# A graph diffusion with a routed feed-forward layer: the order of loads, stores and zeroing in SyncE's queue

## The chip, the cores and the metric

The kernel runs on one core of one Trainium2 chip. The metric is the device time of one execution in microseconds; of the kernel before, three runs are shown, and one further execution was recorded by the hardware profiler. Engines: PE is TensorE, DVE is VectorE, ACT is ScalarE, POOL is GpSimd, SP is SyncE. SP computes nothing here: it reads a few registers and issues most of the DMAs, strictly in the order of its queue.

## The reference

There are 3125 rows (nodes) of 256 numbers and 103,125 edges. First a linear graph diffusion of six steps, then a layer of eight experts, of which each row uses two. Cut to what matters:

```python
x = x + gnn(layernorm(x))          # silu(h @ W_in.T + b_in), 6 diffusion steps, @ W_out.T + b_out
xn = layernorm(x) * gamma + beta
top_vals, top_idx = top_k(xn @ Wr + br, 2)
w = softmax(top_vals)
for e in range(8):
    h = gelu(xn @ W1[e] + b1[e])   # 256 -> 512
    y = y + (h @ W2[e] + b2[e]) * w_full[..., e, None]
x = x + y
```

One diffusion step is `term = segment_sum(term[src], dst) * inv_deg / i`, and the six terms and the start are added up.

## The kernel before, in words

**First step.** The edges are made into a dense matrix of 25 row blocks of 128 x 3200 (`build_tile`, L647 to L687): DVE compares, PE multiplies (`pa`), ACT writes the block, and SP copies it to DRAM (`adj`, L686). In the same loop (L718) each block is multiplied with the start vector (`pd`, L727), and `finish` scales and adds. `last`, what `finish` returns, is an instruction of DVE.

In the first ten rounds of this loop SP also issues a DMA that writes 640 KB of zeros into the DRAM tensor `ys` (`nought`, L721): `ys` has one row of results for each of the two experts of each node, and every row that is read later must hold a number. These DMAs wait for nothing in the loop, and the scheduler that puts the instructions of each engine in order has set them ahead of the first block's copy.

**Steps two to six** (L1106): the blocks come back from DRAM one by one, and PE multiplies them, 25 blocks a step.

**Routing.** During the last step each block of 128 rows is normalised, the two best experts are found, and POOL scatters the row twice into the DRAM tensor `xs`, a list for each expert (`route`, L900). `lists_end` cuts the lists into pieces of 256 rows, 27 pieces in all, and orders them so that pieces whose rows come early in the node order come first.

**The experts' stage** (`experts`, L1017, called at L1130). Piece i passes through these steps:

- `load(i)` (L1024): SP reads the piece's first row and its expert into registers, and issues five DMAs: `xr` (256 rows and, in a 257th column, the row of `ys` for each result; 257 KB), `w1_sb` and `w2_sb` (512 KB each), `b1_sb` (2 KB) and `b2_sb` (128 KB). These tiles have three buffers each, so xr of piece i+2 can be loaded when nothing reads xr of piece i-1 any more. The last reader is the scatter of piece i-1, which takes its row numbers from it.
- `turned`: PE transposes the piece into `px` (L1045), DVE copies it to `xt` (L1048).
- `hidden`: PE multiplies with W1 into `ph` (L1056), ACT applies gelu (L1058).
- `results`: for each half of 128 rows PE multiplies with W2 into `py` (L1065), DVE adds the bias into `y` (L1068; three buffers), and POOL scatters the 128 rows into `ys` (L1069).

The loop at L1077 stands in this order: hidden(i), turned(i+1), results(i), load(i+2). PE's order in a round is thus `ph` of i, `px` of i+1, `py` of i.

**Sums.** `READY` (L57) names four checkpoints: before piece 10 the results of the nodes' blocks 0 to 4 are complete, before piece 16 those of blocks 5 to 9, before piece 21 blocks 10 to 14, before piece 24 blocks 15 to 19. If the order of the pieces doesn't allow it, a flag (`rare`) is set and all is done again behind the stage. In the rounds of the checkpoints `results_of` (L994) loads the five blocks' results, two DMAs of 640 KB (`got0`, `got1`; L1000). It reads `ys`, which the scatters write. The scatters among themselves are told apart by `dram_disjoint_views`; the load of `got` is not, so it waits for all scatters before it in the program, and the next scatter behind it in the program waits for the load. `summed` (L1008) then does two DVE instructions for a block (L1011, L1013) and a store to the output (L1015), two blocks a round in rounds that are no checkpoint. Blocks 20 to 24 are loaded when the last piece is done (4 whole blocks and the last of 53 rows, so four DMAs), and their stores are shared by SP and ACT.

The order of each engine's queue is set by a scheduler that looks at readiness. `tc.issue_after(ins)` is a block in which every instruction that goes to the queue of `ins`'s own engine is put behind `ins` in that queue; it makes no wait, and it says nothing about other engines.

## Time and profile before

| what | us |
|---|---|
| three runs: median (lowest to highest) | 1333.0 (1332.65 to 1334.83) |
| the profiled execution | 1329.78 |
| its span, first to last instruction | 1328.0 |
| mean granted clock of TensorE | 0.971 of full |
| PE busy | 1231.4 (93%) |
| DVE busy | 622.2 (47%) |
| ACT busy | 347.4 (26%) |
| POOL busy | 115.5 (9%) |
| `pd` of steps two to six (L1121), PE busy | 713.5 |
| `py` (L1065) and `ph` (L1056), PE busy | 100.4 and 99.4 |
| `ys<-nought`, ten DMAs of 640 KB, issue to landing | 10.4 (median) |
| `got<-ys`, eight DMAs of 640 KB, issue to landing | 5.8 (median) |
| `xr<-xs`, 27 DMAs of 257 KB, issue to landing | 2.8 (median) |

The page says for each engine how long it was busy, for each group of instructions how often it ran and what ended the idle time before it, and for each DMA how long it took from issue to landing. A share of busy time is a mean over stages with different limits. The views of the trace say more: the waits of an engine and who ended them, the timeline of a stretch, and for a stretch the busy times, the clock that TensorE was granted (PEclk, 1.00 is full) and what the DMA engines moved. Where an instruction waits for several things the profile names the one that came last by its own reckoning, which can be the wrong one.

### The profile page before, as it was taken

Reading aid. Unit: us, or ns where it says so; the run is one execution under the profiler, and the core shown is the slowest. Engines: PE = TensorE matmul, PEld = TensorE weight load, DVE = VectorE, ACT = ScalarE, POOL = GpSimd, SP = SyncE. Lnnn points to the kernel's source line nnn. Section 1 sums busy time; section 2 is a strip of 40 time slices with the busy share of each in tenths; the row PEclk is TensorE's granted clock in tenths of the full one; section 3 lists DMA queues with packets and bytes.
Section 4 is the critical chain, followed back from the end, with each engine's and each line's share of the span. In section 5 each row is a group of like instructions: output and inputs, shape, how many; then the busy total and the mean of one; then the engine's idle time right before and its main releaser. Section 6 shows DMA issues by size and latency. Waiting matters only on the chain. (4 is left out here: it accounts for less than half of the span.)

```text
span 1328.0 us, 16605 instructions
## 1 busy us (share of the span) xinstructions
PE 1231.4 (93%) x6190; PEld 1017.5 (77%) x6190; DVE 622.2 (47%) x1587; ACT 347.4 (26%) x534; POOL 115.5 (9%) x141
## 2 busy tenths in 40 slices
PE   3899999998999999999999999999999829998983
PEld 2678888887888888888888888887777618877872
DVE  5759999995344443333222222236555422122232
ACT  4656676664000000000000000002222202222220
POOL 2000000000000000000000000000333222221221
PEclk9899999999999999999999999999999959999996
DMA  9204444345988888888888888887888276787892
GB/s 302 95 11 192 190 165 196 159 202 227 357 292 294 293 292 295 293 293 295 295 295 295 296 294 297 297 291 276 289 288 287 89 187 223 223 254 252 256 297 99
DMA packets 91059, 326.08 MB, mean 246 GB/s; under 512 B 12013, under 2 KB 61052, under 8 KB 71768
## 3 DMA queue, kind: packets, MB, share of 16 engines
q1 hardware_dynamic: 82588, 307.71, 65.2%
q0 software_dynamic: 5280, 14.54, 3.3%
q10 hardware_dynamic: 3100, 2.66, 0.7%
q8 instruction: 51, 0.84, 0.2%
q14 instruction: 40, 0.33, 0.1%
HBM read 256.44 MB, written 67.63 MB: 244 GB/s over the span
## 5 line engine op out<-in xcount | busy, mean ns | idle before, releaser
L1121 PE MATMUL pd<-t,blk 128*128 128x512 f32 (+1 forms) x3125 | 713.5, 388 | 4.0 <-DMA blk<-adj 4.0
L1121 PEld LDWEIGHTS pd<-t,blk 128*128 128x128 f32 x3125 | 575.2, 188 | 121.8 <-issue 4.3
L695 DVE SCALAR_TENSOR_TENSOR term<-pd,inv_deg,low 128x256 f32<-128x256 f32 x150 | 72.4, 482 | 406.2 <-ACT low L693 406.0
L693 ACT ACTIVATE low<-pd,inv_deg 128x256 f32<-128x256 f32 x150 | 71.2, 475 | 642.5 <-PE pd L1121 575.5
L681 ACT CAST blk<-pa 128x800 fp32r<-128x800 f32 x98 | 146.5, 1645 | 12.1 <-PE pa L677 12.1
L727 PE MATMUL pd<-t,blk 128*128 128x512 f32 x625 | 145.9, 389 | 0.0
L727 PEld LDWEIGHTS pd<-t,blk 128*128 128x128 f32 x625 | 115.4, 188 | 23.3
L666 DVE TENSOR_TENSOR right<-steps,place 128x800 bf16<-128x800 f16 (+3 forms) x245 | 128.1, 579 | 3.3 <-PE pa L677 3.3
L1065 PE MATMUL py<-w_sb,ht 128*128 128x256 f32 x432 | 100.4, 387 | 0.0
L1056 PE MATMUL ph<-xt,w_sb 128*128 128x256 f32 x432 | 99.4, 383 | 0.8 <-DVE xt L1048 0.8
L677 PE MATMUL pa<-right,left 128*128 128x200 bf16 (+3 forms) x980 | 98.9, 254 | 0.9 <-ACT blk L681 0.9
L677 PEld LDWEIGHTS <-left 128*128 128x128 bf16 x980 | 83.4, 97 | 13.8 <-issue 4.6
L1056 PEld LDWEIGHTS ph<-xt,w_sb 128*128 128x128 f32 x432 | 83.0, 193 | 12.7 <-DVE xt L1048 1.2
L1058 ACT ACTIVATE ht<-ph,b_sb 128x256 f32<-128x256 f32 x108 | 50.9, 474 | 158.5 <-PE ph L1056 153.6
L1065 PEld LDWEIGHTS py<-w_sb,ht 128*128 128x128 f32 x432 | 82.1, 195 | 10.6
L657 DVE TENSOR_TENSOR left<-steps,lane 128x2560 bf16<-128x2560 f16 x49 | 72.8, 1485 | 1.2 <-PE pa L677 1.1
L769 POOL IOTA lane_f<- 128x1 f32 x1 | 0.1, 138 | 840.7 <-PE pd L1121 840.7
L1069 POOL DMA_INDIRECT ys<-y,xr x54 | 53.0, 982 | 175.9 <-DVE y L1068 106.0
L1048 DVE COPY xt<-px 128x512 f32<-128x512 f32 x27 | 18.6, 691 | 97.0 <-PE px L1045 78.8
L900 POOL DMA_INDIRECT xs<-xg,to x50 | 48.9, 977 | 104.5 <-DVE m L839 37.9
L701 DVE TENSOR_TENSOR acc<-acc,term 128x256 f32<-128x256 f32 x125 | 52.5, 420 | 0.9
L1068 DVE TENSOR_TENSOR y<-py,b_sb 128x256 f32<-128x256 f32 x54 | 22.9, 424 | 61.2 <-PE py L1065 61.0
(233 smaller groups left out, 606.9 us busy)
## 6 DMA issues: line engine op xcount, KB each, us to landing
blk<-adj SPq DMA_DIRECT2D x125, 1600.0 KB, 6.7
adj<-blk SPq DMA_DIRECT2D x25, 1600.0 KB, 5.2
w_sb<-in_w_dram SPq DMA_DIRECT2D x54, 512.0 KB, 5.5
xr<-xs SPq DMA_DIRECT2D x27, 257.0 KB, 2.8
ys<-nought SPq DMA_DIRECT2D x10, 640.0 KB, 10.4
got<-ys SPq DMA_DIRECT2D x8, 640.0 KB, 5.8
b_sb<-in_b_dram SPq DMA_DIRECT2D x27, 128.0 KB, 5.2
out_dram<-got SPq DMA_DIRECT2D x22, 128.0 KB, 5.2
```

Of the source, the lines that this page charges most:

```text
L657: nc.vector.tensor_tensor(left.rearrange("p k a l u -> p (k a) l u"), steps[:, None, :P, :].to_broadcast([P, nl, P, 2]), lane[:, h, :, :]. ...
L666: nc.vector.tensor_tensor(r, steps[:, None, :m, :].to_broadcast([P, HALF // 2, m, 2]), place[:, h, k, :].rearrange("p (a u) -> p a u", u=2 ...
L677: nc.tensor.matmul(pa[:, u, lo * NT:hi * NT], left[:, k, a, :, u], right[k][:, a, :, u], start=(k == 0), stop=(k == CK - 1), skip_group_ch ...
L681: nc.scalar.copy(by_dst[:, q:q + 2 * W, :].rearrange("p (u q) i -> p u q i", u=2), pa[:, :, :W * NT].rearrange("p u (q i) -> p u q i", i=NT))
L693: nc.scalar.activation(low, pd[:, D:], AF.Copy, scale=inv)
L695: put = nc.vector.scalar_tensor_tensor(term, pd[:, :D], inv, low, op0=ALU.mult, op1=ALU.add)
L701: put = nc.vector.tensor_add(acc[:, j, :], acc[:, j, :], term)
L727: nc.tensor.matmul(pd[:, :n], blk[:, i * P:(i + 1) * P], t0[:, i, :n], start=(i == 0), stop=(i == NT - 2), skip_group_check=True)
L1056: nc.tensor.matmul(ph, got[1][:, k, q * P:(q + 1) * P], xt[:, k, :], start=(k == 0), stop=(k == 1))
L1065: nc.tensor.matmul(py, ht[:, q, h * P:(h + 1) * P], got[2][:, q, :], start=(q == 0), stop=(q == HT - 1))
L1069: nc.gpsimd.indirect_dma_start(ys_at[2 * min(i, NSLOT) + h], bass.IndirectOffsetOnAxis(ap=got[0][:, h, D:].bitcast(U32), axis=0), y, None)
L1121: nc.tensor.matmul(pd[:, :n], blk[:, i * P:(i + 1) * P], old[:, i, :n], start=(i == 0), stop=(i == NT - 2), skip_group_check=True)
```

## The change

There are four parts.

1. In the first step the zeroing DMAs move from rounds 0 to 9 to rounds 2 to 11, and stand in a block `tc.issue_after(last.ins)`.
2. In the experts' loop `load(i + 2)` moves from the end of the round to its start, and the loads of results at a checkpoint come next, ahead of hidden(i). `load` also returns its last DMA (of `b2_sb`), and `results` its last DVE addition (`y`).
3. The sums of a round stand in two order blocks: the DVE part behind `y` of the round, the stores on SP behind the last DMA of the newest load.
4. Blocks 20 to 24 are loaded in pairs (20 and 21, 22 and 23, 24 alone), `got0` from SP's queue and `got1` from ACT's, and the sums of a pair follow its loads.

```diff
     for j in range(NT):
-        if j < 10:
+        if 2 <= j < 12:
             n = 2 * YK // 10
-            nc.sync.dma_start(ys[j * n:(j + 1) * n, :].rearrange("(a p) d -> p a d", p=P),
-                              nought[:, None, :].to_broadcast([P, n // P, D]))
+            with tc.issue_after(last.ins):
+                nc.sync.dma_start(ys[(j - 2) * n:(j - 1) * n, :].rearrange("(a p) d -> p a d", p=P),
+                                  nought[:, None, :].to_broadcast([P, n // P, D]))
...
-    def results_of(sums, a, b):
+    def results_of(sums, a, b, on=(nc.sync, nc.sync)):
...
-            nc.sync.dma_start(
-                got[:, :full - a, :],
-                ys[k * YK + a * P:k * YK + full * P, :].rearrange("(t p) d -> p t d", p=P))
+            if full > a:
+                on[k].dma_start(
+                    got[:, :full - a, :],
+                    ys[k * YK + a * P:k * YK + full * P, :].rearrange("(t p) d -> p t d", p=P))
             if full < b:
-                nc.sync.dma_start(got[:LAST, full - a, :], ys[k * YK + full * P:k * YK + N, :])
+                on[k].dma_start(got[:LAST, full - a, :], ys[k * YK + full * P:k * YK + N, :])
...
-                nc.sync.dma_start(b2_sb, b2[ds(e, 1), :].to_broadcast([P, D]))
-                return xr, w1_sb, w2_sb, b1_sb, b2_sb
+                d = nc.sync.dma_start(b2_sb, b2[ds(e, 1), :].to_broadcast([P, D]))
+                return xr, w1_sb, w2_sb, b1_sb, b2_sb, d.ins
...
-                for i in range(a, b):
-                    ht = hidden(got[0], xt)
-                    if i + 1 < b:
-                        xt = turned(got[1])
-                    for n, t in READY if sums else ():
-                        if i == n:
-                            both = results_of(sums, gone, t)
-                            left += [(both, gone, q) for q in range(gone, t)]
-                            gone = t
-                    results(i, got[0], ht)
-                    got = got[1:]
-                    if i + 2 < b:
-                        got.append(load(i + 2))
-                    if i not in [n for n, _ in READY]:
-                        for one in left[:2]:
-                            summed(*one, nc.sync)
-                        left = left[2:]
-                if sums:
-                    both = results_of(sums, gone, NT)
-                    for one in left:
-                        summed(*one, nc.sync)
-                    for q in range(gone, NT):
-                        summed(both, gone, q, nc.scalar if q % 2 else nc.sync)
+            for i in range(a, b):
+                if i + 2 < b:
+                    got.append(load(i + 2))
+                for n, t in READY if sums else ():
+                    if i == n:
+                        both = results_of(sums, gone, t)
+                        left += [(both, gone, q) for q in range(gone, t)]
+                        gone = t
+                ht = hidden(got[0], xt)
+                if i + 1 < b:
+                    xt = turned(got[1])
+                y = results(i, got[0], ht)
+                got = got[1:]
+                if i not in [n for n, _ in READY]:
+
+                    with tc.issue_after(y.ins), tc.issue_after(got[-1][-1] if got else y.ins):
+                        for one in left[:2]:
+                            summed(*one, nc.sync)
+                    left = left[2:]
+            if sums:
+                for one in left:
+                    summed(*one, nc.sync)
+                for q in range(gone, NT, 2):
+                    both = results_of(sums, q, min(q + 2, NT), (nc.sync, nc.scalar))
+                    for t in range(q, min(q + 2, NT)):
+                        summed(both, q, t, nc.scalar if t % 2 else nc.sync)
```

The arithmetic is the same. Every DMA of before is there with its size, except that the last results are cut into pairs.

More of the change, by code (lines that the diff above doesn't have):

```diff
@@ L1067, in results @@
                     y = ffn.tile([P, D], F32, name="y")
-                    nc.vector.tensor_add(y, py, got[4])
+                    put = nc.vector.tensor_add(y, py, got[4])
                     nc.gpsimd.indirect_dma_start(
@@ L1071, in results @@
                         bass.IndirectOffsetOnAxis(ap=got[0][:, h, D:].bitcast(U32), axis=0), y, None)
-            got, gone, left = [], 0, []
-            if True:
-                got = [load(i) for i in range(a, min(a + 2, b))]
-                xt = turned(got[0])
-                for i in range(a, b):
-                    ht = hidden(got[0], xt)
-                    if i + 1 < b:
-                        xt = turned(got[1])
-                    for n, t in READY if sums else ():
-                        if i == n:
-                            both = results_of(sums, gone, t)
-                            left += [(both, gone, q) for q in range(gone, t)]
-                            gone = t
-                    results(i, got[0], ht)
-                    got = got[1:]
-                    if i + 2 < b:
-                        got.append(load(i + 2))
-                    if i not in [n for n, _ in READY]:
+                return put
@@ new lines, in experts @@
+            gone, left = 0, []
+            got = [load(i) for i in range(a, min(a + 2, b))]
+            xt = turned(got[0])
+            for i in range(a, b):
[13 more added lines that the diff above has]
+                    with tc.issue_after(y.ins), tc.issue_after(got[-1][-1] if got else y.ins):
```

## The prediction

> **What bounds the kernel now.** I read the page first: PE is busy for 93% of the span, but the chain of waits reaches back only to 1077.8 us, so the diffusion before it is PE from end to end. Then the sums per stretch: from 1089.9 (first `ph`) to 1306.0 (end of the last `py`) stands the experts' stage, 27 pieces of 256 rows. Then the waits of that stage, and the timeline at the first place where PE stops in it.

> ```profile
> span 1328.0 us, 16605 instructions
> ...
> PE px L1045 <- DMA xr<-xs: 29.9, 5, 17.6
> ```

> The second line is from the waits (in all, times, longest): 17.6 us are the start of the stage, the other 12.3 us are four stops, at pieces 12, 18, 23 and 26, each the piece loaded just behind a pair of `got` loads. The timeline at the first (start, duration, engine; in brackets the idle time before it and its releaser):

> ```profile
> 1168.52 0.60 PE L1045 MATMUL px<-ident,xr 128*128 128x128 f32 x4
> ...
> 1171.53 0.95 SPq L1000 DMA_DIRECT2D got<-ys  x2
> ...
> 1172.68 0.38 SPq L1030 DMA_DIRECT2D xr<-xs  x1
> ...
> 1178.68 1.00 POOL L1069 DMA_INDIRECT ys<-y,xr  x1 [11.75 <-DVE got L1011]
> ...
> 1178.79 1.09 PE L1045 MATMUL px<-ident,xr 128*128 128x128 f32 x4 [2.76 <-DMA xr<-xs]
> 1179.67 4.62 PE L1065 MATMUL py<-w_sb,ht 128*128 128x256 f32 x16
> ...
> 1183.85 0.38 SPq L1030 DMA_DIRECT2D xr<-xs  x1
> ...
> 1187.58 0.60 PE L1045 MATMUL px<-ident,xr 128*128 128x128 f32 x4
> ```

> Two things are to be seen. First, SP waits for the scatter of piece 9 (landed 1171.48), issues `got`, and only then xr of piece 12, which lands behind 1.3 MB, 2.9 us too late. Second, the scatter of piece 10, whose y was ready at 1171.3, goes out at 1178.68: it writes `ys`, which the `got` loads read, so it waits until they have landed. The row names a DVE instruction, but got1 (6.0 us from its issue at 1171.96) had landed at 1177.96, and at all four places POOL starts 0.7 to 0.9 us after got1 lands. In the built programs, before and after alike, that scatter waits for both `got` loads. And xr of piece 13 (1183.85) waits for that scatter, since it takes its buffer.

> PE's undisturbed step is 7.345 us ((1168.52 - 1102.41)/9, `px` to `px`). Against it the four places lose: piece 10's 2.93 + 1.45 (px 12 and then px 13), piece 16's 3.70, piece 21's 3.07, piece 24's 3.34 + 1.69 = **16.2 us** in all. The 1.45 and 1.69 are TensorE at half clock. Windows (PE busy, PEclk, DMA share, GB/s):

> ```profile
> 1174.87:1178.28 3.41, 1.16 (x6) 1.00 1.09 363
> 1178.28:1181.69 3.41, 2.90 (x9) 0.50 1.04 342
> 1226.07:1229.48 3.41, 1.50 (x9) 1.00 1.07 365
> ```

> After a stretch of 3.41 us with 1.16 us of PE work the next is at 0.50; after one with 1.50 it is not.

> **The change, part by part.**

> *Zeroing.* The ten `nought` DMAs are put into an order block behind `last`, a DVE instruction. Such a block orders only what is queued on that instruction's own engine, and these are on SP. In the built order they stand where they stood, places 9 to 18 of SP's queue, with the same waits. 0 us. (Had they moved, the gathers beside them, 6.2 and 7.2 us to landing, could at best come near the 2.4 us of a quiet scatter: some 4 us each.)

> *Loads ahead of `got` at pieces 10, 16 and 21.* SP is released at the same moment S (1171.53, 1220.99, 1260.35), because load(i+2) waits for the same scatter as `got` did. xr lands at about S + 2.8 (median of all xr), before its need at S + 4.3, 3.3, 4.5: the stop at px 12, 18 and 23 goes. What is late next is the scatter held by `got`. `got` now follows five loads (1.41 MB). In all 2.76 MB flow; the rows

> ```profile
> 1171.50:1174.00 2.50, 2.50 (x13) 2.19 (x13) 0.00 (x0) 0.47 (x1) 0.00 (x0) 1.00 0.39 82
> 1174.00:1177.90 3.90, 2.03 (x10) 1.45 (x8) 1.85 (x5) 1.42 (x3) 0.00 (x0) 1.00 1.09 367
> ```

> say 0.2 MB in the first 2.5 us and then 0.365 MB/us: 2.5 + 7.0, and 0.2 to land, so got1 lands at **S + 9.7** (before: S + 6.4). Ends: 8.5 if the queue's transfers overlap more than in the rows; 10.4, when the last of the same transfers landed before (1181.9). Then the chain, each step from a row of before: +0.8 POOL's release, +1.3 to the scatter's second half (1178.68 to 1179.99), +2.7 its landing (2.4/2.7/3.4 around 1270), +0.1 issue, +2.7 xr (2.7 and 2.6 at 1232 and 1272), +0.1 to PE: px of piece 13, 19, 24 at **S + 17.4**. Undisturbed they are due at 1183.21, 1231.65 and 1272.20. Late by 5.7, 6.7, 5.6 = 18.0 us. In the built order two of the eight matmul pairs of `py` stand ahead of exactly these three `px`, and fill 0.86 us of each stop (3.46/4): 15.4 us.

> *Half clock.* Each of these stops leaves PE idle for 4.7 to 5.9 us. [...] the rows show 1.45 and 1.69, and PE may come back in mid-window: I take 1.5, ends 0.6 and 2.4. Three times: 4.5 us.

> So pieces 10, 16, 21 cost 15.4 + 4.5 = 19.9 us, where they cost 4.4 + 3.7 + 3.1 = 11.1: **+8.8 us**.

> *Piece 24.* No load follows piece 26's, so nothing waits for the held scatter on PE's side: px 26 comes in time, and 5.0 us go. Part comes back on DVE and POOL: got1 lands at about S + 10.9 (S = 1284.62; there the last load of the set landed at S + 11.8), the scatter of 24 goes out at S + 11.7 and lands 3 us later, y of 25 (second half) waits for its buffer until then, two tiles' sums (4 x 0.43) stand before y of 26, and the last scatter lands at about S + 22.5, before at S + 26.0 (1310.65). **-3.5 us**, ends -1.5 and -5.

> *Sums behind y and the load, stores behind.* In the order block they do stand there. SP's stores wait for sums that end about 2 us after y, and the load behind them waits for a scatter until about 3 us later: hidden. At the end SP's last two stores wait for sums that end about 2 us after y of 26, and the scatter needs 4.2 us: hidden; if not, some 0.5 us.

> *Last tiles in pairs, half of them from ACT's queue.* The tail's row:

> ```profile
> 1312.14 9.15 DMA got<-ys
> ...
> 1316.00:1319.50 3.50, 0.00 (x0) 0.00 (x0) 1.54 (x5) 0.00 (x0) 0.00 (x0) 0.50 0.07 23
> ```

> For 3.5 us the DMA moves 23 GB/s, where 2 us earlier it moved over 340: the two 53-row loads run on one DMA engine, and the final sum waits for the second. The change starts whole tiles sooner, but these 109 kB stay. [...] Were ACT's 53 rows on another engine, 54 kB/23 GB/s = 2.4 us would go, and the row cannot exclude it. I take 0, ends -3 and +1.

> **Sum**: 8.8 - 3.5 + 0 = +5.3 us. The profiled execution is 1329.78 us (span 1328.0 and 1.8 around it), so 1335.1; the median of the runs shown is 3.2 us higher, at 1333.0, and there it is **1338 us**.

> **Rivals.**
> *The held scatter comes free earlier.* If the `got` bytes pass between the loads instead of behind them, got1 lands by S + 7.5. Then px 13, 19 and 24 are 3.5, 4.5 and 3.4 us late, less 2.6 for the `py` in front: 8.8, and with one drop of the clock 10.3, against 11.1. With -3.5: **1329 us**, faster. It decides where got1 lands before about S + 8. For it: scatters did land between loads. Against: before, xr landed 0.7 us after got1 at piece 10, 257 kB at 0.365 MB/us, as in one line.
> *The stops simply go.* -16.2 + 1.5 at piece 24: **1318 us**. It needs a scatter that doesn't wait for `got`; four held scatters (1178.68, 1227.97, 1267.88, 1293.23) speak against it.
> *The clock stays down longer.* Two windows at half rate at each stop, and got1 at S + 10.4: +2.1 and +4: **1344 us**.
> That the zeroing isn't moved is in the sum already.

> **Chances.** Slow chain (1334 to 1342) 0.62; clock down longer 0.10; scatter free earlier 0.18; stops gone 0.06; moved zeroing or a tail on two engines on top, 0.04. What a measurement can tell from no change is 0.2%, 2.7 us. Slower 0.68, within 0.16, faster 0.16. The range takes in the early scatter and most of the long clock: 1328 to 1344.

> **What would show it.** Right: idle before px 13, 19 and 24 of some 5 us, released by xr, none at 12, 18, 23 and 26; POOL's scatter of pieces 10, 16, 21 some 3 us later than before, counted from S; PEclk 0.50 after each stop. Wrong: these scatters within 8 us of S, or a stop elsewhere; zeroing issued after 60 us; the 23 GB/s stretch gone from the tail.

## The result and the profile after

| | us |
|---|---|
| kernel before, four runs: median (lowest to highest) | 1332.83 (1330.45 to 1334.83) |
| changed kernel, four runs | 1347.32 (1344.43 to 1348.32) |
| ratio, 95% interval | 1.0106 (1.0083 to 1.0129) |
| span of the profiled execution, before and after | 1328.0 and 1346.0 |
| granted clock of TensorE, before and after | 0.971 and 0.963 |

The change makes the kernel 1.1% slower. Lines of the changed kernel lie two or more higher than before's: `got` is L1002, `xr` L1032, `px` L1047, `py` L1067, `y` L1070, the scatter L1071. First two of the waits in the profile after (in all, times, longest):

```profile
PE px L1047 <- DMA xr<-xs: 39.9, 4, 18.3
DVE y L1070 <- DMA ys<-y,xr: 29.5, 5, 9.1
```

PE's wait was 29.9 us in five places before. Of the 39.9 us, 18.3 are the start of the stage, so three stops hold 21.6 us where four held 12.3. The timeline around the first of them (start, duration, engine; in brackets the idle time before it and what ended it):

```profile
1173.35 0.38 SPq L1032 DMA_DIRECT2D xr<-xs  x1
...
1176.16 1.00 SPq L1002 DMA_DIRECT2D got<-ys  x2
...
1177.83 0.60 PE L1047 MATMUL px<-ident,xr 128*128 128x128 f32 x4
...
1185.18 1.03 PE L1067 MATMUL py<-w_sb,ht 128*128 128x256 f32 x4
...
1187.06 0.96 POOL L1071 DMA_INDIRECT ys<-y,xr  x1 [18.16 <-DMA got<-ys]
1188.32 0.96 POOL L1071 DMA_INDIRECT ys<-y,xr  x1 [0.31 <-issue]
1189.58 0.42 DVE L1070 TENSOR_TENSOR y<-py,b_sb 128x256 f32<-128x256 f32 x1 [8.95 <-DMA ys<-y,xr]
...
1190.83 0.38 SPq L1032 DMA_DIRECT2D xr<-xs  x1
...
1193.77 1.09 PE L1047 MATMUL px<-ident,xr 128*128 128x128 f32 x4 [7.57 <-DMA xr<-xs]
```

The load of piece 12 now goes first (at S = 1173.35, when SP is released), and `px` of piece 12 at 1177.83 has no bracket: the old stop is gone. `got` follows at 1176.16, and its second half, `got1`, lands at 1186.29. Only then can POOL scatter piece 10 (1187.06), when its second half has landed SP can reload that piece's `xr` buffer (1190.83), and `px` of piece 13 stands at 1193.77 where it was due at 1185.18.

The held scatter keeps a second thing, which the prediction saw only at piece 24: the buffers of `y`. There are three of them, and DVE stands 8.95 us before `y` of piece 11's second half (1189.58), 29.5 us in five places in all; before, DVE has no such wait. It ends before `px` of piece 13 and so does not set the stop here.

Now the stretches of that checkpoint, first two for the DMA, then five in steps of 3.41 us for the clock, which falls at 1188.46 and rises at 1198.70, three such steps apart (length, busy time of PE, PEld, DVE, ACT, POOL, then PEclk, DMA share, GB/s):

```profile
1178.00:1180.50 2.50, 2.50 (x15) 2.24 (x14) 0.99 (x2) 0.47 (x1) 0.00 (x0) 1.00 0.81 254
1183.00:1186.50 3.50, 3.21 (x15) 2.47 (x13) 0.00 (x0) 1.74 (x4) 0.00 (x0) 1.00 0.20 66
1185.10:1188.51 3.41, 1.11 (x6) 0.62 (x4) 0.00 (x0) 0.47 (x1) 1.15 (x2) 0.99 0.01 5
1188.51:1191.92 3.41, 0.00 (x0) 0.00 (x0) 2.00 (x5) 0.00 (x0) 2.80 (x3) 0.50 0.33 117
1191.92:1195.33 3.41, 1.56 (x6) 1.50 (x7) 0.43 (x1) 0.00 (x0) 0.10 (x1) 0.50 0.98 302
1195.33:1198.74 3.41, 3.41 (x9) 2.69 (x9) 0.68 (x2) 0.00 (x0) 0.96 (x1) 0.51 0.93 264
1198.74:1202.15 3.41, 3.41 (x17) 3.00 (x17) 2.00 (x5) 1.06 (x3) 0.96 (x1) 1.00 1.05 349
```

The transfers run at 254 GB/s and end in a tail of 66 GB/s, where before's rows had 363 to 367. And three stretches, not one, are at half clock, two of them with PE at work; at the other two stops it is three and two.

### The profile page after: what moved, and what is told of

Its sections match the earlier page's. It is cut to its first block, busy times and chain, and to the rows that moved or that the text cites. A ratio compares the mean times of both kernels' runs of the same rounds, so it can differ in the third digit from the quotient of the medians.

```text
span 1346.0 us, 16605 instructions
## 1 busy us (share of the span) xinstructions
PE 1235.1 (92%) x6190; PEld 1020.8 (76%) x6190; DVE 623.0 (46%) x1587; ACT 347.5 (26%) x534; POOL 114.9 (9%) x141
## 5 line engine op out<-in xcount | busy, mean ns | idle before, releaser
L681 ACT CAST blk<-pa 128x800 fp32r<-128x800 f32 x98 | 146.5, 1647 | 12.1 <-PE pa L677 12.1
L1067 PE MATMUL py<-w_sb,ht 128*128 128x256 f32 x432 | 103.7, 395 | 0.0
L1067 PEld LDWEIGHTS py<-w_sb,ht 128*128 128x128 f32 x432 | 84.3, 200 | 11.4
L1071 POOL DMA_INDIRECT ys<-y,xr x54 | 52.6, 974 | 195.9 <-DVE y L1070 96.5
L1070 DVE TENSOR_TENSOR y<-py,b_sb 128x256 f32<-128x256 f32 x54 | 22.9, 425 | 88.0 <-PE py L1067 58.4
L1047 PE MATMUL px<-ident,xr 128*128 128x128 f32 x108 | 18.5, 297 | 39.9 <-DMA xr<-xs 39.9
## 6 DMA issues: line engine op xcount, KB each, us to landing
ys<-nought SPq DMA_DIRECT2D x10, 640.0 KB, 10.5
```

What stands on the lines that cost most here:

```text
L681: nc.scalar.copy(by_dst[:, q:q + 2 * W, :].rearrange("p (u q) i -> p u q i", u=2), pa[:, :, :W * NT].rearrange("p u (q i) -> p u q i", i=NT))
L1067: nc.tensor.matmul(py, ht[:, q, h * P:(h + 1) * P], got[2][:, q, :], start=(q == 0), stop=(q == HT - 1))
L1071: nc.gpsimd.indirect_dma_start(ys_at[2 * min(i, NSLOT) + h], bass.IndirectOffsetOnAxis(ap=got[0][:, h, D:].bitcast(U32), axis=0), y, None)
```

## The experiments

They ran in five sets, each with the kernel before beside them: e1 to e4; e5, e6, e7 and after_again; e8, e9, e10 and e6_again; e11 and e12; e13. The kernel before took 1352, 1329, 1333, 1353 and 1349 us, and in the three sets near 1350 the experts' stage begins some 18 us later. Why is not shown; it is not the chip alone, since 1329 and 1353 bear the same chip number. So each time is given as a ratio to the kernel before in the same set.

### The changed kernel again, and the order alone

**after_again** is the changed kernel, unchanged, beside others of these runs.

> The changed kernel as it is, for a profile and a ratio on the same chip as the others: ratio 1.0106 within 0.002, stops at px 13, 19, 24 of 6.4 to 7.7 us, got1 landing at S + 12.5 to 13.3.

Ratio 1.0114 (1.0098 to 1.0131); `px` 13, 19 and 24 are 9.0, 8.2 and 7.3 us late; from S to the held scatter it takes 14.0, 12.8 and 12.5 us.

**e1_got_first**: only the order at a checkpoint is put back.

```diff
-                if i + 2 < b:
-                    got.append(load(i + 2))
                 for n, t in READY if sums else ():
...
+                if i + 2 < b:
+                    got.append(load(i + 2))
```

> The changed kernel, with one thing undone: at a checkpoint the two loads of results stand ahead of load(i+2) again. Theory (the results behind the load land late, the scatter of the checkpoint's piece waits for them, and load(i+3) waits for that scatter): the idle of PE moves back from px of pieces 13, 19, 24 (7.6, 7.6, 6.4 us) to px of 12, 18, 23, 26 (about 2.9, 3.7, 3.1, 3.3 us), the scatter goes out about S + 7 instead of S + 13.7, and the time is that of the kernel before, 1333 (1329 to 1337). Rival (the other parts, zeroing, order of the sums, tail in pairs, cost some of the 14.5 us): the time stays above 1340.

Ratio 0.9995 (0.9982 to 1.0008). Its timeline at the first checkpoint:

```profile
1191.37 0.95 SPq L1002 DMA_DIRECT2D got<-ys  x2
...
1192.52 0.38 SPq L1032 DMA_DIRECT2D xr<-xs  x1
...
1198.54 0.96 POOL L1071 DMA_INDIRECT ys<-y,xr  x1 [11.75 <-DMA got<-ys]
...
1198.64 0.63 PE L1047 MATMUL px<-ident,xr 128*128 128x128 f32 x4 [2.76 <-DMA xr<-xs]
```

Here S is the issue of `got` (1191.37). The scatter is held for 7.2 us from it, and the stop is back at `px` 12, 18, 23 and 26. The whole loss comes from the order of loads and results; order of the sums, tail in pairs and the zeroing as written come to nothing together, within 0.2%.

### Is it the hold, or the traffic?

**e3_got_from_x**: the same bytes at the same place in the queue, but from a tensor that no scatter writes (the sums of these blocks are left without the experts' results).

```diff
-                    ys[k * YK + a * P:k * YK + full * P, :].rearrange(
+                    (x[a * P:full * P, :] if a < 20 else
+                     ys[k * YK + a * P:k * YK + full * P, :]).rearrange(
...
-                        both = results_of(sums, gone, t)
+                        with tc.issue_after(got[-1][-1]):
+                            both = results_of(sums, gone, t)
```

> The changed kernel, but the loads of results of blocks 0 to 19 read the same rows of the kernel's input x instead of ys, in the same places of SyncE's queue: the same bytes in the same shape, and no scatter waits for them (the sums of these blocks are left without the experts' results). Theory (hold): scatters go out as soon as y is there, no stop at px 13, 19, 24, time 1318 (1312 to 1323). Rival (contention of the transfers): stops stay within 2 us of their size, time above 1340. For the late landing of the second load: if it lies in the traffic alone, it lands again at about S + 12.5 to 13; if it has to do with ys (rows just written), at S + 10 or less.

Ratio 0.9923 (0.9897 to 0.9950). Applied to 1332.8 us that is 1322.6, at the upper end of the theory's range; but its "no stop" is wrong. The timeline:

```profile
1189.74 0.96 POOL L1072 DMA_INDIRECT ys<-y,xr  x1 [4.66 <-DVE y L1071]
...
1193.18 1.49 SPq L1002 DMA_DIRECT2D got<-in_x_dram  x2
...
1197.77 0.38 SPq L1033 DMA_DIRECT2D xr<-xs  x1
...
1204.94 0.88 DVE L1016 SCALAR_TENSOR_TENSOR got<-got,g,got 128x256 f32<-128x256 f32 x2 [1.62 <-DMA got<-in_x_dram]
...
1205.73 1.09 PE L1048 MATMUL px<-ident,xr 128*128 128x128 f32 x4 [4.20 <-DMA xr<-xs]
```

Piece 10's scatter goes out as soon as `y` is there (1189.74, no hold), and SP reloads its `xr` at 1197.77, 6.3 us behind the scatter's second half (1191.47), as in the round before. Still piece 13 is late, with a stop of 4.2 us: its 257 KB need 8 us from issue instead of 2.8. The results stand in front of them and the weights behind, and from 1197 to 1206 the DMA engines are busy nearly throughout (2.86 MB, 318 GB/s). The three stops together are 7.8 us, against 21.4 in after_again (in another set). So the hold makes about two thirds of the stops; the rest goes with the traffic that `got` puts ahead of load(i+3), and would stay in this order if the scatter went free.

The run answers a second question. The sum that waits for `got1` starts at 1204.94, S + 14.6 (S = 1190.36), and at S + 13.1 and S + 13.4 at the next two checkpoints. So the late landing does not need rows of `ys` that have just been written: it is there when `x` is read (though here the next load's bytes flow beside it).

### Taking the hold away

**e2_rows_out** copies the row numbers out of `xr`, so that the scatter no longer keeps `xr`'s buffer; `y` and the copy get six buffers. That takes away both holds at once, and no run here separates them.

```diff
                 nc.vector.tensor_copy(xt, px)
-                return xt
+                at = outs.tile([P, 2], U32, name="at")
+                nc.vector.tensor_copy(at, got[0][:, :, D].bitcast(U32))
+                return xt, at
...
-                    y = ffn.tile([P, D], F32, name="y")
+                    y = outs.tile([P, D], F32, name="y")
...
-                        bass.IndirectOffsetOnAxis(ap=got[0][:, h, D:].bitcast(U32), axis=0), y, None)
+                        bass.IndirectOffsetOnAxis(ap=at[:, h:h + 1], axis=0), y, None)
```

> The changed kernel, but DVE copies the two columns of row numbers out of xr into a tile of their own, and y and this tile have six buffers: xr's buffer no longer waits for the scatter. Theory (hold through xr's buffer): the scatter of pieces 10, 16, 21 still waits for the results' loads, but no px stands idle for more than 0.5 us after piece 2, PEclk stays 1.00 between 1110 and 1300, and the 22.1 us of delay and 6.9 us of half clock go: 1347.3 - 29 = 1318 (1312 to 1323), faster than both. Rival (the load of piece 13 is late because the DMA engines are busy with the results): a stop of 3 us or more stays at px 13, 19 or 24, and the time stays above 1330.

Ratio 0.9949 (0.9929 to 0.9968): faster than before, but the 1318 us would have been 0.989. DVE's waits say why:

```profile
DVE at L1052 <- DMA xr<-xs: 104.4, 22, 15.5
```

The copy needs nothing but `xr`, so the scheduler set it ahead of `y` of earlier pieces, and DVE stood there until a later piece's `xr` landed: 22 times, 104 us. The hold had moved to DVE.

**e6_rows_behind** puts the copy directly behind the same piece's `xt`.

```diff
-                nc.vector.tensor_copy(xt, px)
+                done = nc.vector.tensor_copy(xt, px)
                 at = outs.tile([P, 2], U32, name="at")
-                nc.vector.tensor_copy(at, got[0][:, :, D].bitcast(U32))
+                with tc.issue_after(done.ins):
+                    nc.vector.tensor_copy(at, got[0][:, :, D].bitcast(U32))
```

> As e2_rows_out, but the copy of a piece's row numbers stands in DVE's queue directly behind the copy of the same piece's px, which needs the same load. Theory (in e2 the scheduler set the copy of a later piece ahead of y, and DVE stood there until that piece's xr landed; xr's hold itself is gone): no DVE wait for xr of more than 0.3 us, no stop of px or ph above 0.5 us except in the first three pieces, and the stage falls by the stops of before (16 us): ratio to before 0.987 to 0.990. Rival (loads behind the results' transfers still come late, as in e3 where px 13 stood 4.4 us without any hold): stops of 1.5 us or more stay at px 13, 19 or 24, ratio 0.992 or more.

Ratio 0.9876 (0.9857 to 0.9895); a second time, as **e6_again**:

> e6_rows_behind once more, beside e10 and e9 on one chip: ratio 0.9876 within 0.002.

0.9879 (0.9852 to 0.9907). From piece 3 to 26 every `px` follows the one before by 7.35 us. The timeline of e6_rows_behind at the first checkpoint:

```profile
1166.46 0.38 SPq L1032 DMA_DIRECT2D xr<-xs  x1
...
1169.53 0.95 SPq L1002 DMA_DIRECT2D got<-ys  x2
...
1170.71 0.38 SPq L1034 DMA_DIRECT2D w_sb<-in_w_dram  x1
...
1176.68 0.96 POOL L1075 DMA_INDIRECT ys<-y,at  x1 [10.30 <-DVE xt L1050]
...
1182.67 0.60 PE L1047 MATMUL px<-ident,xr 128*128 128x128 f32 x4
```

The scatter is still held until `got` has landed (it goes out 6.8 to 7.2 us behind `got`'s issue at the first three checkpoints; the row names a DVE instruction, but in e1 the same delay ends with `got`), but nobody waits for it. And SP's queue has moved up by a piece: the `xr` at 1166.46 is piece 13's, ahead of `got`, its weights follow `got` (1170.71), and its `px` at 1182.67 is in time. That is how the traffic found in e3 costs nothing here. It also ends the late landing: in the changed kernel, with five loads directly in front of `got`, the scatter went out 9.6 to 11.1 us behind its issue.

**e9_first_rows** is e1_got_first with the same copy: is the change's order needed for this gain?

> e1_got_first (results' loads ahead of load(i+2)) with the row numbers copied out of xr as in e6. It asks whether e6's gain belongs to the freed buffer alone or needs the order of the change. Theory (with the hold gone, load(i+2) still stands behind the results, which wait for the scatter at S): px 12, 18, 23, 26 stand idle for about 3 us each as in before, ratio 0.995 to 1.001. Rival (the freed buffer alone does it): no stop above 1 us, ratio 0.987 to 0.990.

Ratio 0.9865 (0.9838 to 0.9893), and no stop either: the rival is right. Its timeline has `xr` of piece 13 at 1169.64 and `got` at 1172.93. With the buffer free, the scheduler sets that load ahead of the results by itself.

| ratio to before | results first in the program | load first in the program (the change) |
|---|---|---|
| `xr` and `y` held by the scatter | e1: 0.9995 | after_again: 1.0114 |
| row numbers copied out, six buffers of `y` | e9: 0.9865 | e6: 0.9876 and 0.9879 |

The second row does not compare two orders. In SP's queue e6 and e9 are alike at the first three checkpoints: `xr` of piece 13 (19, 24), the results, then that piece's weights. The results behind all five loads with both holds gone was not run; the nearest is e3, with 7.8 us of stops.

### Why the second load of results lands so late

My sum had the held scatter of pieces 10, 16 and 21 at S + 10.5 us. The mean over these three places is 13.3 in the profile after and 13.1 in after_again (12.4 to 14.0 one by one). **e4_bias_first** moves the biases ahead of the weights:

```diff
+                b1_sb = ffn.tile([P, HT], F32, name="b1_sb")
...
                 w1_sb = ffn.tile([P, 2, H], F32, name="w1_sb")
```

> The changed kernel, but in a load the two biases (2 KB in rows of 16 bytes, and one row of 1 KB read 128 times) are issued behind xr and ahead of the weights. It asks why the second load of results lands at S + 12.9 and not S + 9.7. Theory A (the slow stretch of 80 to 280 GB/s belongs to the biases' packets, which the results stand behind): the stretch moves to just behind xr, and the weights still land late; if the total is the same, got1 lands at S + 12 to 13 all the same. Theory B (it is the results standing behind the broadcast row that is slow): got1 lands at S + 10 to 11 and the time falls by 5 to 8 us, to 1340. Theory C (the results' own start behind any transfer is slow): stretch stays at got0's start, S + 12.9, time within 3 us of 1347.

Ratio 1.0189 (1.0161 to 1.0217). Two stretches of an ordinary round of it, without results:

```profile
1185.00:1187.50 2.50, 2.50 (x15) 2.19 (x15) 0.00 (x0) 1.38 (x4) 0.40 (x1) 1.00 0.68 108
1187.50:1190.00 2.50, 2.50 (x13) 2.21 (x13) 1.12 (x2) 0.16 (x1) 0.00 (x0) 1.00 1.00 359
```

Behind the biases the DMA moves 108 GB/s for 2.5 us, a like stretch stands in most rounds, and the weights land late: `ph` waits for them in ten places, 12.3 us in all. The slow stretch belongs to the biases, as theory A had it, but the scatter of piece 10 goes out at S + 14.1, so moving it ahead saves nothing. The next runs change one thing each:

- **e5_b2_rows**: 128 copies of each row of b2 in DRAM, one row for each partition.

```diff
+                    nc.sync.dma_start(b2x, b2[:, None, :].to_broadcast([NE_X, P, D]))
...
-                d = nc.sync.dma_start(b2_sb, b2[ds(e, 1), :].to_broadcast([P, D]))
+                d = nc.sync.dma_start(b2_sb, b2x[ds(e, 1)].rearrange("a p d -> p (a d)"))
```

> The changed kernel, but the bias row b2 of each expert is first written 128 times into a DRAM tensor (one DMA of 1 MB in the second diffusion step), and the load of b2_sb reads 128 different rows of it instead of one row 128 times. Theory (all DMA engines reading one row of DRAM are slow, and what stands behind waits): behind the biases no packets of 1 KB take over 100 ns any more, got1 lands 2 to 3 us sooner, S + 10 to 11, the stops at px 13, 19, 24 become 4.5 to 5.5 us, and the kernel is 6 to 10 us faster than the changed one on the same chip (ratio to before 1.003 to 1.006). Rival (the start of the results' own reads, or the 16-byte rows of b1, is what is slow): stretch and stops stay, ratio 1.0106 within 0.002.

- **e8_biases_out**: e5 without the loads of b1.

```diff
-                b1_sb = ffn.tile([P, HT], F32, name="b1_sb")
-                nc.sync.dma_start(b1_sb, b1[:, ds(e * HT, HT)])
+                b1_sb = b1_one
```

> e5_b2_rows without the load of b1 as well (128 rows of 16 bytes each piece; the b1 of expert 0 is loaded once and used for all, so seven experts' first bias is left out). What is open: got1 landed at S + 13 with both biases and about 1.3 us sooner without the broadcast row; my sum had S + 9.7. Theory (the small rows of b1 cost the rest): no slow stretch is left behind w2, got1 lands by S + 10, ratio to before 1.000 to 1.005. Rival (the results' own first reads, and w2's, are slow whatever stands before them): got1 at S + 10.8 to 12, ratio 1.007 to 1.011.

- **e11_got_near**: e5 with the results' rows 2 KB apart in each partition.

```diff
+                    ys[k * YK + a * P:k * YK + a * P + 2 * S * P, :].rearrange(
+                        "(p t u) d -> p t u d", p=P, u=2)[:, :, 0, :] if a < 20 and b == a + S else
```

> e5_b2_rows with other rows of ys in the loads of results of blocks 0 to 19: each partition reads five rows of 1 KB that lie 2 KB apart, not 128 KB apart; packets, bytes, places and waits are the same (the sums of these blocks take the wrong rows). From S to the scatter of the checkpoint's piece it took 13.3 to 13.5 us in the changed kernel, 12.1 in e5, and 10.5 in my sum. Theory (rows 128 KB apart[...]): the results' first packets take 50 ns and not 70 to 140, the scatter goes out at S + 11.0 to 11.5. Rival (a start behind other transfers is slow whatever the addresses): S + 11.9 to 12.4.

- **e12_w2_near**: e11, with w2's rows 2 KB apart.

```diff
-                nc.sync.dma_start(w2_sb, w2[ds(e, 1)].rearrange("a (q p) d -> p (a q) d", p=P))
+                nc.sync.dma_start(w2_sb, w2[0:2].rearrange("a (p q u) d -> p a q u d", p=P // 2, u=2)[:, :, :, 0, :].rearrange("p a q d -> (a p) q d"))
```

> e11_got_near, and w2 is read in the same way, each partition four rows 2 KB apart (always of experts 0 and 1, so the second product uses wrong weights). Theory (as there): no 1 KB packet of w2 takes over 60 ns in the mean of half a microsecond, the load and the results flow at 340 GB/s and more once they run, and the scatter goes out at S + 10.2 to 10.8, my sum. Rival: a stretch under 290 GB/s stays between w2 and the results, S + 11.5 or more.

- **e13_w2_in_place**: e12, with w2's load kept behind w1's (`with tc.issue_after(d.ins)`, where `d` is the load of w1).

> e12_w2_near with the load of w2 held to its place. In e12 the scheduler had issued it a round earlier, since it no longer waited for the expert's number, so 512 KB were missing ahead of the results, and its S + 11.0 to the scatter says nothing on addresses. Here w2 stands behind w1 again (rows 2 KB apart, of experts 0 and 1, so the second product uses wrong weights). Theory (rows 128 KB apart make w2's start slow): the scatter of the checkpoint's piece goes out at S + 10.2 to 11.2, and no stretch of 2.5 us between w2 and the results is under 290 GB/s. Rival (the addresses don't matter): S + 11.7 to 12.4 as in e5 and e11, and a stretch under 290 GB/s stays.

| | S to the held scatter, mean of pieces 10, 16, 21 (us) | ratio to before |
|---|---|---|
| forecast | 10.5 | |
| changed kernel | 13.3 and 13.1 | 1.0106 and 1.0114 |
| e5, b2 from 128 rows | 12.0 | 1.0102 (1.0083 to 1.0121) |
| e8, and no b1 | 12.0 | 1.0083 (1.0055 to 1.0112) |
| e11, results' rows near | 12.2 | 1.0095 (1.0058 to 1.0133) |
| e12, w2 gone from ahead of the results | 11.0 | 1.0013 (0.9996 to 1.0031) |
| e13, w2's rows near, in place | 12.3 | 1.0088 (1.0056 to 1.0121) |

Reading one row 128 times costs the scatter 1.1 to 1.3 us: all three values of e5 (11.7 to 12.3) lie below all six of the changed kernel. The whole kernel's median is 3.0 us below after_again's in the same set, where 6 to 10 had been expected. b1's 128 rows of 16 bytes in a piece cost nothing that shows here: e8, without them, has the 12.0 us of e5. The distance of the rows makes no difference here (12.2 us in e11 and 12.3 in e13). e12 is no test of addresses, since w2, no longer waiting for the expert's number, was issued a round earlier. But it shows the weight of bytes: 0.5 MB fewer ahead of the results, and the scatter is about 1 us sooner in the mean (2.0, 1.7 and -0.3 us against e11). Some 1.5 us stay unexplained. In e13 a part of them looks like this:

```profile
1195.50:1196.50 1.00, 1.00 (x8) 0.90 (x7) 0.18 (x1) 0.47 (x1) 0.00 (x0) 1.00 0.47 117
1196.50:1201.50 5.00, 5.00 (x25) 4.40 (x24) 0.94 (x2) 0.47 (x1) 0.00 (x0) 1.00 1.03 340
```

About where w2 starts, the engines are less than half busy (0.47) for a microsecond, with more transfers in their queue. No run tells why.

**e7_both** joins e6 and e5:

> e6_rows_behind with b2 read from 128 rows as in e5_b2_rows. Theory: if e6 has no stop left, b2 is no longer on any path and the time is that of e6 within 0.2%, ratio 0.987 to 0.990. Rival (the loads are still late behind the results): it is 2 us or more faster than e6.

Ratio 0.9891 (0.9874 to 0.9907), the same as e6 within the intervals: off the path, b2's slow row costs nothing that shows.

### The zeroing, truly moved

**e10_zero_moved** is e6, with the order block behind an instruction of SP's own queue.

```diff
-        nc.sync.dma_start(adj[j], blk.bitcast(F32))
+        copied.append(nc.sync.dma_start(adj[j], blk.bitcast(F32)))
...
-            with tc.issue_after(last.ins):
+            with tc.issue_after(copied[-1].ins):
```

> e6_rows_behind with the zeroing truly moved: each of the ten DMAs of zeros is put behind the copy of the round's block to DRAM, an instruction of SyncE's own queue, where the change named one of DVE, which left them where they were. Theory from the first step's rows (gathers beside the zeroing took 6.2 and 7.2 us to landing, a quiet scatter 2.4): up to 4 us sooner in the tables, of which some is hidden: 0 to 6 us less than e6, ratio 0.983 to 0.988. Rival (the zeroing hid behind the building of the first block anyway, and beside the copies it delays them): same as e6, or slower by up to 5 us.

Ratio 0.9824 (0.9797 to 0.9851), beside 0.9879 for e6_again in the same set: 1310.16 and 1316.91 us against 1333.14 for the kernel before. The list of DMAs (KB each, median us from issue to landing) of e6_again, where the zeros stand where they stood:

```profile
ys<-nought SPq DMA_DIRECT2D x10, 640.0 KB, 10.4
row_i<-in_dst_cm_dram,chunk_i POOLq DMA_INDIRECT x2, 6.1
rec<-edges,start_i POOLq DMA_INDIRECT x2, 7.2
```

and of e10_zero_moved:

```profile
ys<-nought SPq DMA_DIRECT2D x10, 640.0 KB, 7.0
row_i<-in_dst_cm_dram,chunk_i POOLq DMA_INDIRECT x2, 4.9
rec<-edges,start_i POOLq DMA_INDIRECT x2, 5.5
```

The zeros now start at 111.84 us instead of 14.87. The first `pa`, which needs the gathered tables, starts at 49.10 instead of 53.47, and the first `px` at 1085.2 instead of 1089.3: the gain comes in the first step and is kept. (The medians differ by 6.8 us and the profiled executions by 3.0; e10's was its slowest and e6_again's its fastest.) This is the fastest kernel of the study.

## Why the prediction was right and wrong

Direction and mechanism held; the size did not. Forecast were 1338 us, 5 more than before, and the kernel took 14.5 more: 1347.3 lies above the range (1328 to 1344). The steps that failed are two terms of the sum, the landing of `got1` (+6.7 us over the three places) and the half clock behind each stop (+2.4). By its own steps, with the profile after:

- **Zeroing not moved, 0 us**: right. Its ten DMAs start at 14.60 (before 14.71). Had it moved, "some 4 us each" for the gathers was put as the best case; e10 beside e6_again has 1.2 and 1.7 us for them, and 4.4 us at the first `pa`.
- **The stops at `px` 12, 18, 23, 26 go; new ones at 13, 19, 24 released by `xr`**: right.
- **got1 at S + 9.7, ends 8.5 and 10.4**: the step that failed most, as a size. It landed at S + 12.9 at the first checkpoint, and the mean of the three is S + 12.6, outside both ends. I took "2.5 us and then 0.365 MB/us" from rows in which the results ran first. Behind a load they didn't reach this rate: some 1.2 us lie in the bias row that is read 128 times (e5), some 1.5 us in starts and tails whose cause is open. e3 has the late landing too, with `x` read in place of `ys`. The chain behind it was as forecast: from got1's landing to `px` took 7.5 us (1193.77 - 1186.29), in the sum 7.7. So the three `px` came 8.6, 8.7 and 7.5 us late, 24.7 in all and 22.1 after the `py` ahead of them, where the sum had 18.0 and 15.4.
- **Half clock, 1.5 us a stop**: the second term that was too small. The 1.5 came from the 1.45 and 1.69 us of before; its ends, 0.6 and 2.4, were an estimate that no row of before shows. The round after each stop took 8.93, 9.07 and 8.31 us against 6.48 (7.345 - 0.86): 2.45, 2.59 and 1.83, in all 6.9, where the sum had 4.5 (one stretch at half clock for each stop; there were three, three and two). The rival "the clock stays down longer" had 8.5 for it, but got1 at S + 10.4, and so 1344.
- **Pieces 10, 16 and 21, +8.8**: measured 22.1 + 6.9 - 11.1 = +17.9.
- **Piece 24, -3.5, ends -1.5 and -5**: inside its ends. The last scatter landed 23.9 us behind S, before 26.0: -2.1.
- **Tail, 0**: right. From the last scatter's landing to the last of `got` it took 10.6 us in both, and the two loads of 53 rows, now from two queues, still run at one DMA engine's rate (27 GB/s and a DMA share of 0.08 from 1337 to 1339; before, 23 and 0.07). What a second queue does for such loads, no row of before showed; here ACT's queue bought nothing.
- Not in the sum: `px` of piece 2, ahead of the first checkpoint, came 2.0 us later than before, most of it between `px` 0 and `px` 1. These are 7.49 us apart in the profile after, 6.88 in after_again, 6.21 before, 6.28 in e6_rows_behind, and 6.8 to 7.2 in the others (e4, whose weights land late, apart). It varies from run to run; whether the change has a part in it is not settled.

17.9 - 2.1 + 2.0 = 17.8, where the sum had 5.3, and the span grew by 18.0. The medians differ by 14.5, since the profiled execution of before was 3.0 us below its median and that of after 0.5 above its own.

Of the rivals, "the held scatter comes free earlier" fell (`got1` at S + 12.6, not 7.5), and so did "the stops simply go". But e3 shows that even a scatter that is not held would have left a third of the stops, so that rival's 1318 was too low for the reason that it gave; e6 reached this size with `xr` of piece 13 ahead of the results.

## What to carry to other kernels

A transfer that is moved back in a queue takes along everybody who waits for it: before moving it, follow the chain to its end, here results, scatter, buffer, load, `px`. The scatter's wait for the results stayed in every run but e3; the cure was to let nobody wait for the scatter. 1 KB of row numbers had kept a buffer of 257 KB, and three buffers of `y` were too few for a scatter that is held for some 13 us. With the numbers copied out and six buffers of `y`, the scheduler set the next `xr` ahead of the results, whichever order the program had, and no stop was left. How much each of the two did was not tested. When such a copy is added, tie it to the place where its input is known to be there, or the scheduler makes a new wait of it.

In these runs a transfer's duration belonged to its place in the queue: `xr` of 257 KB took 2.8 us in the median before and 8 us behind the results in e3. Take it from a row in which the same transfers run in the same order, and where there is none, let the range say so.

## What the runs showed of the hardware

One row of DRAM read 128 times by one DMA was slow here, together with its neighbours. In e4, where it stands with b1's load, the DMA moved 108 GB/s for 2.5 us, against 359 just behind. Where the results stand behind it, the 2.5 us from S + 5.5 on ran at 174 GB/s in after_again (from 1176.50); in e5, which reads 128 rows, 2.5 us ran at 278 GB/s from S + 4.8 (1177.00) and at 321 from S + 5.8 (1178.00), at the price of one DMA of 1 MB earlier.

What follows of the clock was read from the granted clock (PEclk) in the profiles before and after. Between 1100 and 1300 us it changes at 1178.28, 1181.69, 1294.33 and 1297.74 before, and at 1188.46, 1198.70, 1243.08, 1253.32, 1290.86 and 1297.69 after: within each profile whole multiples of 3.41 us apart, hence the stretches of that length.

The rest of the stage agrees (from 1095 us to 25 us before the end, in stretches of 3.41 us that begin where the granted clock changes, in these two profiles). At full clock, 5 stretches with 1.16 us of PE work or less were followed by half clock, and all 110 with 1.41 us or more by full clock. At half clock, 5 with 1.80 us or less were followed by half clock, and 5 with 2.90 us or more by full. These figures are of this stage's matmuls alone.
